# Five gathers moved within GpSimd's order in the second step of a graph layer

## The chip, the cores and the metric

The kernel runs on one core of a Trainium2 chip. The core has five engines that each work through their own instruction queue: TensorE (PE, matrix products; its weight loads are listed as PEld), VectorE (DVE), ScalarE (ACT), GpSimd (POOL) and SyncE (SP, which here only issues DMAs). Queues wait for one another by semaphores. The metric is the device time of one execution in microseconds (us), the median of several runs.

## The reference

One layer of a graph network on 3327 nodes with 256 features each. `adj` is a sparse 3327 x 3327 matrix with a diagonal.

```python
h = relu(layernorm(x))
R = adj + I;  R = R / R.sum(-1, keepdims=True)
Xf = Xa = h;  Z = 0
for n in range(2):
    A  = top_p_attention(Xa, W1, W2, W3)    # softmax rows; the largest entries up to a sum
    Xf = R @ Xf                             # of 0.9 are kept and scaled to sum 1
    Xa = A @ Xa
    Z  = Z + Xf @ U1[n].T + Xa @ U2[n].T
out = x + layernorm(h + Z) * ln_g + ln_b
```

The costly part is the attention: for each of 3327 rows of 3327 probabilities, the threshold above which the kept entries hold 0.9 of the row's sum has to be found.

## The kernel before, in words

Nodes are cut into NT = 26 tiles of 128 rows (P). The two steps of the reference are the two rounds of the loop `for step in range(2)` (from L1112), and within a step the loop over `i` runs from -1 to 27. In iteration i several tiles are worked on at once, each at another stage. A stage is a Python generator, and each `yield` ends one piece of it. A table of letters says how the pieces are woven: an iteration has seven parts (PARTS), and for each part a string names the stages whose next piece is emitted, letter by letter (L1158, L1159). `PLAN[1]` is the second step's table; `OPEN` replaces it for the first iterations (-1 to 3) and `LAST` for the last ones (25 to 27). The instruction order on PE, ACT and DVE is pinned to the order of this text, and from the start of the second step that of POOL too (L1183 to L1188). SP's is not.

The stages that matter here, in the second step:

- `w`, `q`: `weights`, the logits of a tile (PE, L597) and their exponentials (ACT, L601, L605) into a tile `e` of 128 x 3328.
- `m` and, from the next iteration on, `n`: `measured_twice` for tile i+1, which guesses the threshold (called the guess's chain here). Its pieces: (A) small ACT operations and two on POOL, L673 and L674; (B) a pass over the whole `e` on ACT (`through`, L630); (C) a second such pass; (D, the middle part) DVE L681, L682, ACT L683 to L685, then POOL L686, L687, L688; (E) a third pass on ACT; (F) POOL L693, L694, DVE L695, L696, ACT L698 to L701, DVE L703, L704, POOL L705, L706; (G) ACT L708, an exponential scaled by the column that L706 writes; (H) DVE L710, L711, which write the guess. A to F are emitted in iteration i as `m`, in parts 0, 1, 3, 4, 5 and 6; G and H in parts 1 and 2 of the next iteration as `n`.
- `d`, `c`: `settle` for tile i, on DVE: one operation over the whole tile that compares `e` with the guess (L725), 20 searches for the eight largest of a segment (L730), the search over the candidates (L734 to L749), and one operation over the whole tile that cuts `e` at the threshold (L759). L725 and L759 each read two SBUF inputs and take 3.69 us.
- `g`: `fetching`, the chain of `refetch(t)` over all tiles. For a tile it issues on SP one load of the packed adjacency blocks (`ac`, L1088), and on POOL five indirect DMAs (L897, "gathers") that fetch rows of `vx` into `xg`. Each call of `g` issues one gather, the first one of a tile also the load. `ac` and `xg` have two buffers.
- `s`: `spread` for tile i, which multiplies `ac` with `xg` on PE (L905) and adds on DVE (L1080).
- `f`: `finish`, the layer norm of a finished tile; on POOL L462, L463, L937 (the reciprocal deviation) and, one iteration later, L945 to L947.
- `sums.turn` and `sums.sum` transpose the cut `e` (PE L805, ACT L807) and multiply it with the features (PE L819).

In iterations 4 to 23 the gathers of iteration i are for tile i+2. Twelve gathers are issued in iterations -1 and 0, and in iterations 1 to 3 there is a sixth one in part 5 (`mgdf`), so that the 130 gathers end in iteration 23. POOL's order in an iteration of the second step is: L673, L674, L945 to L947, the five gathers, L686 to L688, L462, L463, L937, L693, L694, L705, L706.

Of the kernel before, what the change touches and what calls it, by code (L numbers as in the profile page):

```python
# [344 lines left out]
def guess_graph_layer(ctx, tc, x, adj, w1t, w2t, w3t, u1t, u2t, ln_g, ln_b, out, flag):  # L345
# [740 lines left out]
    def refetch(t):  # L1086
# [7 lines left out]


    PLAN = (("mdsssa", "mcdsssa", "edawwp", "msda", "mpdea", "gdwwq", "emgq"),
            ("llcmss", "lnms", "lwwnfd", "lcmdsssggggg", "fsmwqdf", "llmdf", "lmwd"))

    LAST = {NT - 1: ("cfss", "cn", "nd", "sss", "fdddddsf", "f", ""), NT: ("c", "", "", "ff", "ff", "fv", "f"),
            NT + 1: ("fv", "f", "", "", "f", "f", "f")}  # L1100
    OPEN = {-1: ("llcmss", "lnms", "lwwnfd", "lcmdsssggggg", "fmgswqdf", "llmdf", "lmwfdm"),
            0: ("cmssggg", "nms", "wwnfd", "cmdsss", "fsmgwqdf", "mdf", "mwd"),
            1: ("cmss", "nms", "wwnfd", "cmdsssggggg", "fsmwqdf", "mgdf", "mwd")}
    OPEN[2] = OPEN[3] = OPEN[1]
    fetching = itertools.chain(*(refetch(t) for t in range(NT)))
    LATE = (1, 4)
# [81 lines left out]
@with_exitstack  # L1188
def tile_graph_layer(ctx, tc, *args):
    keep = ctx.enter_context(tc.tile_pool(name="keep", bufs=1))  # L1190
    flag = keep.tile([1, 1], I32, tag="flag", name="flag")
    guess_graph_layer(tc, *args, flag)
    failed = tc.nc.values_load(flag[0:1, 0:1], min_val=0, max_val=1 << 20)
    with tc.If(failed > 0):
        search_graph_layer(tc, *args)
# [34 lines left out]
```

## Time and profile before

| | |
|---|---|
| median of 3 runs | 1404.44 us (1404.25 to 1408.04) |
| the profiled execution: its time / its span | 1405.77 us / 1404.0 us |
| mean granted TensorE clock | 0.981 |
| busy share of the span: PE, DVE, ACT, POOL | 91%, 85%, 79%, 57% |
| the 130 gathers of the second step (L897, `xg<-vx`) | 129.5 us busy, 996 ns each; idle before them 38.6 us |
| L673 in the second step, 23 occurrences with `law` | 46.4 us busy, 2017 ns each |
| L686, 25 occurrences | 267 ns each |
| L693, 25 occurrences | 258 ns each |
| L725 and L759 on the whole tile | 3.69 us each |

Lines of the profile read: an engine, the source line, the operation, output and inputs with their shapes, and a count; in the time line, the start in us from the beginning of the span, the length, and in brackets how long the engine sat idle before it and what ended that wait. "issue" is a time in which the engine waited for nothing that the profile shows. The chain of waits is the work that ended last, followed back from the end.

### The profile page before, as it was taken

The numbers are of one execution on the slowest core, as the hardware profiler recorded it, in microseconds if no ns is written. First come the engines' busy times: TensorE is split into PE (matmuls) and PEld (weight loads), VectorE is DVE, ScalarE is ACT, GpSimd is POOL, SyncE is SP. The second block draws the span as 40 slices with busy tenths as digits, with TensorE's granted clock in tenths as the row PEclk, the third lists the DMA queues.
The fourth block names the chain that finished last, engine by engine and source line by source line (L and its number), as shares of the span: only waits on it lengthen the run. The fifth ranks groups of instructions, "written<-read, shape, count | busy, mean of one in ns | idle before, by whom it ended". The sixth has DMA issues, their size and how long they took to land.

```text
span 1404.0 us, 22095 instructions
## 1 busy us (share of the span) xinstructions
PE 1275.7 (91%) x6495; PEld 976.9 (70%) x6495; DVE 1195.0 (85%) x3673; ACT 1105.3 (79%) x2451; POOL 795.3 (57%) x1243
## 2 busy tenths in 40 slices
PE   6897999999999999999999759999999999999985
PEld 5545777777767777777777537777777777777764
DVE  6878898898988979989882489999998999999993
ACT  5467777878877778778773689999998999999941
POOL 6225766666657656666673475655655555565522
PEclk9999999999999999999999879999999999999998
DMA  8884453444444534534422121322312223132200
GB/s 279 269 269 122 118 145 109 128 138 117 128 125 115 143 107 122 146 111 125 126 78 83 51 72 45 90 77 60 91 56 80 67 70 88 50 89 73 63 20 22
DMA packets 91203, 149.77 MB, mean 107 GB/s; under 512 B 15266, under 2 KB 58657, under 8 KB 91073
## 3 DMA queue, kind: packets, MB, share of 16 engines
q1 hardware_dynamic: 73616, 105.37, 23.8%
q0 software_dynamic: 16640, 42.69, 12.3%
q8 instruction: 54, 0.88, 0.3%
q14 instruction: 77, 0.62, 0.1%
q10 hardware_dynamic: 816, 0.20, 0.1%
HBM read 120.93 MB, written 27.28 MB: 106 GB/s over the span
## 4 chain that ended last, share of the span: by engine, by line
PE 43%; DVE 40%; ACT 11%; issue 4%; DMA 1%; POOL 1%; SPq 0%; another core or an unknown queue 0%; DVEq 0%; ACTq 0%; POOLq 0%
PE pa L819 18%; DVE cand L730 8%; DVE w L725 7%; PE pt L805 6%; DVE e L759 5%; PE pr L905 4%; PE pl L597 4%; DVE cand L739 3%; ACT ja L630 3%; DVE bb L737 3%; PE pz L982 3%; PE pz L918 3%; DVE x L759 2%; ACT eT L807 2%; PE pk L1023 1%
## 5 line engine op out<-in xcount | busy, mean ns | idle before, releaser
L819 PE MATMUL pa<-xw,eT 128*128 128x256 f32 x1352 | 323.6, 384 | 27.4 <-DVE s L929 26.2
L630 ACT ACTIVATE ja<-e,g 128x3328 uint8<-128x3328 f32 x106 | 325.7, 3073 | 0.1
L819 PE MATMUL pa<-x,eT 128*128 128x256 f32 x1352 | 325.2, 382 | 0.0
L819 PEld LDWEIGHTS pa<-xw,eT 128*128 128x128 f32 x1352 | 250.7, 190 | 77.9 <-DVE s L929 31.6
L807 ACT COPY eT<-pt 128x512 f32<-128x512 f32 (+1 forms) x364 | 200.6, 559 | 119.8 <-PE pt L805 100.5
L819 PEld LDWEIGHTS pa<-x,eT 128*128 128x128 f32 x1352 | 244.8, 192 | 26.3
L730 DVE MAX8 cand<-w 128x8 f32<-128x168 f32 (+1 forms) x1040 | 251.4, 317 | 0.0
L805 PE MATMUL pt<-ident,e 128*128 128x128 f32 x1144 | 176.1, 276 | 18.2 <-DVE e L756 9.1
L897 POOL DMA_INDIRECT xg<-bx,index x130 | 156.6, 1205 | 45.2 <-issue 31.5
L805 PEld LDWEIGHTS pt<-ident,e 128*128 128x128 f32 x1144 | 140.9, 144 | 57.7 <-issue 29.2
L725 DVE SCALAR_TENSOR_TENSOR w<-e,g 128x3328 f32<-128x3328 f32 x44 | 162.1, 3684 | 0.7
L888 POOL DMA_INDIRECT ac<-in_adj,index x130 | 130.3, 1002 | 44.5 <-issue 29.6
L897 POOL DMA_INDIRECT xg<-vx,index x130 | 129.5, 996 | 38.6 <-issue 38.6
L759 DVE SCALAR_TENSOR_TENSOR e<-e,rec 128x3328 f32<-128x3328 f32 x40 | 147.5, 3688 | 0.6
L905 PE MATMUL pr<-xg,ac 128*128 128x257 f32 (+1 forms) x520 | 140.6, 395 | 6.8 <-DVE s L1080 6.8
L601 ACT ACTIVATE e<-pl 128x832 f32<-128x832 f32 x132 | 113.8, 867 | 17.9 <-PE pl L597 14.4
L905 PEld LDWEIGHTS pr<-xg,ac 128*128 128x128 f32 x520 | 94.0, 194 | 32.1 <-issue 14.2
L737 DVE MAX8 bb<-cand 128x8 f32<-128x160 f32 x286 | 92.6, 324 | 6.4
L597 PE MATMUL pl<-after,qT 64*128 64x416 f32 x416 | 95.5, 553 | 0.0
L597 PE MATMUL pl<-both,qT 64*128 64x416 f32 x416 | 90.4, 538 | 0.8 <-DVE both L1000 0.8
L673 POOL TENSOR_SCALAR g<-g,law 128x1 f32<-128x1 f32 x23 | 46.4, 2017 | 67.4 <-ACT g L672 67.4
L922 POOL TENSOR_TENSOR sv<-sv,x 128x256 f32<-128x256 f32 x26 | 19.8, 763 | 109.9 <-ACT sv L921 109.9
(255 smaller groups left out, 2153.5 us busy)
## 6 DMA issues: line engine op xcount, KB each, us to landing
at<-in_adj SPq DMA_DIRECT2D x102, 256.0 KB
cx<-ac SPq DMA_DIRECT2D x26, 384.0 KB
ac<-cx SPq DMA_DIRECT2D x26, 384.0 KB
wide<-in_adj SPq DMA_DIRECT2D x10, 832.0 KB
e<-in_adj SPq DMA_DIRECT2D x8, 832.0 KB
bx<-e SPq DMA_DIRECT2D x26, 128.5 KB
own<-bx SPq DMA_DIRECT2D x26, 128.5 KB
x<-in_x SPq DMA_DIRECT2D x13, 256.0 KB
```

What stands on the lines that cost most here:

```text
L597: PE.matmul(pl[:, a, :wd], qT[p, :], keys_of(step, a).rearrange("p a b -> p (a b)")[:, c : c + wd], start=True, stop=True)
L630: S.activation(ja, e, f, bias=guess, scale=sign, accum_out=total)
L725: V.scalar_tensor_tensor(w, e, col(16), e, ALU.is_lt, ALU.mult, accum_out=d2)
L730: V.max(cand[:, 8 * s : 8 * s + 8], w[:, s * SEG : min(NP, (s + 1) * SEG)])
L737: V.max(b8, cand)
L759: V.scalar_tensor_tensor(e, e, at(1), e, ALU.is_ge, ALU.mult, accum_out=ra)
L805: PE.transpose(pt[:, j, :], e[:, (j0 + j) * P : (j0 + j + 1) * P], ident)
L807: S.copy(eT[:, :w, :], pt[:, :w, :])
L819: PE.matmul(self.pa, eT[:, c - 4 * k, :], self.xa[:, j, :], start=c == 0, stop=c == NT - 1)
L888: G.indirect_dma_start(out=ac[:, k, :], out_offset=None, in_=rows, in_offset=bass.IndirectOffsetOnAxis(ap=index[:, t, k : k + 1], axis=0), ...
L897: G.indirect_dma_start(out=xg[:, k, :w], out_offset=None, in_=rows, in_offset=bass.IndirectOffsetOnAxis(ap=index[:, t, k : k + 1], axis=0))
L905: PE.matmul(pr[:, :w], ac[:, k, :], own if k == KT - 1 else xg[:, k, :w], start=k == 0, stop=k == KT - 1)
```

## The change

The letters of the second step's table are rearranged. In `PLAN[1]` and in `OPEN[1]` (which also serves iterations 2 and 3) five `g` leave the end of part 3 and stand in part 4 behind `fsm`, that is behind piece D of the guess's chain. Nothing is added or taken away.

```diff
     PLAN = (("mdsssa", "mcdsssa", "edawwp", "msda", "mpdea", "gdwwq", "emgq"),
-            ("llcmss", "lnms", "lwwnfd", "lcmdsssggggg", "fsmwqdf", "llmdf", "lmwd"))
+            ("llcmss", "lnms", "lwwnfd", "lcmdsss", "fsmgggggwqdf", "llmdf", "lmwd"))
...
-            1: ("cmss", "nms", "wwnfd", "cmdsssggggg", "fsmwqdf", "mgdf", "mwd")}
+            1: ("cmss", "nms", "wwnfd", "cmdsss", "fsmgggggwqdf", "mgdf", "mwd")}
```

POOL's order in an iteration becomes: L673, L674, L945 to L947, L686 to L688, the five gathers, L462, L463, L937, L693, L694, L705, L706. The load of `ac`, which comes with a tile's first gather, moves with it in the text. The sixth gather of iterations 1 to 3 stays in part 5.

## The prediction

> **What bounds the kernel now.** I read the page's account by engine first, then the chain of waits, then the time line of one iteration of the second step. The chain over the whole span says that no single engine sets the time:
>
> ```profile
> PE 43%; DVE 40%; ACT 11%; issue 4%; DMA 1%; POOL 1%; SPq 0%; another core or an unknown queue 0%; DVEq 0%; ACTq 0%; POOLq 0%
> ```
>
> In the second step (from 787 us on) the chain runs on VectorE (DVE) with short visits to ScalarE (ACT). VectorE's two long operations and the one wait in between carry an iteration, here the chain's five longest pieces between 1010 and 1032 us:
>
> ```profile
> 1010.83 2.32 DVE cand L730 x10
> 1015.99 0.55 issue
> 1020.46 3.71 DVE e L759 x2
> 1024.88 3.71 DVE w L725 x2
> 1029.57 1.96 DVE cand L730 x8
> ```
>
> The period, from one L682 to the next (1010.61 to 1032.46), is 21.85 us. Of 22 us there PE is busy 20.96, ACT 21.01, DVE 20.47 and POOL (GpSimd) 12.31: three engines are nearly full and GpSimd has slack, but GpSimd's order is that of the text, so what counts is who is late behind what. The same iteration in the time line (start, length, engine, line):
>
> ```profile
> 1010.61 0.21 DVE L682 TENSOR_SCALAR g<-g,oa 128x1 f32<-128x1 f32 x1
> 1011.66 0.29 ACT L685 ACTIVATE g<-g 128x1 f32<-128x1 f32 x1
> 1014.66 0.95 POOL L897 DMA_INDIRECT xg<-vx,index  x1 [0.30 <-issue]
> 1015.66 0.26 POOL L686 TENSOR_SCALAR g<-g 128x1 f32<-128x1 f32 x1
> 1016.30 0.21 ACT L630 ACTIVATION_READ_ACCUMULATOR ja<-x,g 128x1 f32 x1
> 1016.61 0.25 POOL L462 TENSOR_SCALAR rstd<-mv 128x1 f32<-128x1 f32 x1
> 1016.61 0.27 DVE L695 TENSOR_SCALAR g<-oa,g 128x1 f32<-128x1 f32 x1 [0.62 <-issue]
> ...
> 1017.98 0.26 POOL L693 TENSOR_SCALAR g<-oa 128x1 f32<-128x1 f32 x1
> 1019.11 0.30 POOL L706 TENSOR_SCALAR g<-g 128x1 f32<-128x1 f32 x1
> 1020.46 3.69 DVE L759 SCALAR_TENSOR_TENSOR e<-e,rec 128x3328 f32<-128x3328 f32 x1
> 1022.39 1.97 POOL L673 TENSOR_SCALAR g<-g,law 128x1 f32<-128x1 f32 x1 [2.98 <-ACT g L672]
> 1022.46 0.29 ACT L708 ACTIVATE g<-g 128x1 f32<-128x1 f32 x1
> 1024.45 0.23 POOL L674 TENSOR_SCALAR g<-g 128x1 f32<-128x1 f32 x1
> 1024.58 0.27 DVE L711 TENSOR_SCALAR g<-g 128x1 f32<-128x1 f32 x1
> ```
>
> Three things are to be seen. First, L686 is ready when L685 ends (1011.95) but runs at 1015.66: the gathers in front of it cost it 3.7 us. That lateness is nearly free, since L695, which needs L686's column, starts 0.10 us after the accumulator read that ends the third pass (1016.51), and 0.69 us after L686's end: the pass releases it, not GpSimd. Second, GpSimd finishes the chain's last operation (L706, ends 1019.41) 1.05 us before VectorE begins L759. Third, L673, a 128x1 operation, takes 1.97 us when it falls under L759 and ends only 3.90 us after L759's start. The same line took 0.34 us at 791.02, clear of it, and averages 2.02 us over 23 occurrences: a small GpSimd operation that falls under the long two-input operation is held to its end.
>
> **The change, part by part.** Nothing is added or removed: five gathers (and the one load of `ac` on SP's queue that goes with the first) move in the text from ahead of L686-L688 to behind them. It applies to iterations 1 to 23, 23 of them (with 12 gathers issued before and six each in iterations 1 to 3, the 130 run out in iteration 23).
>
> *L686-L688 earlier.* They gain 3.7 us, worth nothing while the third pass releases L695. Only one iteration differs: at 1055.75 a gather began 2.65 us late, L686 ran at 1061.91 and L695 waited 2.52 us instead of 0.63. There the change gains 1.9 us in all.
>
> *The load on SP and the landing of the gathers.* A tile gathered in iteration i is read in iteration i+2, over a period later; both move some 3.5 us later. Cost nothing; the cover is over 20 us.
>
> *What now stands behind the gathers.* Two groups are queued after them: L462, L463, L937 (needed by L944 at 1028.34, 10 us after L937 ends) and L693, L694, L705, L706. L706 scales the exponential L708 on ScalarE, and behind L708 in ScalarE's order stand two 3.07 us passes of the next tile. I count from the end of L682 (1010.82 = 0):
>
> L686 at 1.24 (L685 ends at 1.13; where L686 is not queued it starts 0.11 after, 800.62 to 800.73). L688 0.60 later. First gather 0.53 after L688's start (801.33 to 801.86). Then 1.40 to the second, 3 x 1.255 to the fifth, 1.00 to the next operation (1009.50, 1010.90, 1014.66, 1015.66). L462 so starts at 8.53. L462 to L693 is 1.37: L693 at 9.90. L759 starts at 9.64 (1020.46), so L693 misses it by 0.26 us and is held: to 9.64 + 3.90 = 13.54. L694 0.09 later, 13.63, and 1.07 from there to L706's end (1018.34 to 1019.41): 14.70. L708 starts at 14.81 where it was at 11.64 (1022.46): 3.17 us late.
>
> What is late next: on VectorE, L711 waits for L708, at 15.14 instead of 13.76, 1.38 us. On ScalarE all is back to back from L708 to the end of the second pass of the next tile, 9.53 us (1022.46 to 1031.99): 24.34. Then L681 0.10 later and 0.45 to L682's end: 24.89. VectorE alone would be at L681 at about 22.9, so ScalarE decides. The new period is 24.89, **3.04 us more** than 21.85. PE has 4 us idle then and sets nothing.
>
> The spacing is the delicate choice. The Trainium skill (Perfetto Trace Analysis, GPSIMD Engine Instruction) says that reported spans of GpSimd do not add up and that the start-to-start spacing is to be used. The row shows both: 0.95 us long, 1.255 us apart. By spans the lengths from L686 to L706 add to 7.90 us, end at 9.14, before L759, and the change would cost nothing; by spacing they end at 11.33 without a hold. I go by spacing, since a start is when the next one really came.
>
> *Where the trace has no row* is a L693 that comes under L759 itself. Bounds: not held at all, L706 ends at 11.33 and L708 isn't late (0 us); held as L673 in all 23 occurrences, 3.04 us. L673 is the same kind (tensor-scalar, 128x1), so the upper end. Also unknown is which operation meets L759 first. If one is slower by 0.1 us it is L937 (+0.35 us a period); if the gathers come 1.1 us later it is L462, then 1.40 us more (L463 at 13.63 and 2.47 to L706's end, 16.10). That is what I take for iterations 2 and 3, where a sixth gather goes ahead of L462: 2 x 1.40 = 2.8. In the other direction, L759 could come later by waiting for a running GpSimd operation, at most the 0.26 us of L937.
>
> A second rule concerns gathers themselves. By the Trainium skill (SBUF — State Buffer, Who interferes with whom) a two-input VectorE operation takes only the shared read side, and descriptor writing is inferred not to be hindered by it. Here the gather that began at 851.41 under L725 (849.98 to 853.71) took 3.13 us instead of 0.95, though the one at 850.05 took 1.05. The row decides: gathers that slip under L759 would be held too. By the rule that would save up to 2.1 us in an iteration where it happens; in the forecast no whole gather lies there.
>
> **Sum.** 23 x 3.04 = 69.9; + 2.8; - 1.9: 70.8 us. The profiled execution took 1405.77 (span 1404.0), which gives 1476.6; the median of the runs is 1404.44, 1.3 less, so 1475.2. **I predict 1475 us**, 5.0% slower. A difference of 0.3% (4 us) is about what a measurement can tell from none.
>
> **The rivals.** *Not held, no change.* If a 128x1 operation that starts under L759 were not stopped, L706 ends at 11.33 and ScalarE reaches L708 at 11.64 as before; only the 1.9 us come back: 1402.5, the same. This decides as long as L706 ends before about 11.5. Against it: L673 ends 3.90 us after the start of L759 wherever it falls there; for it: only 0.26 us separate L693 from escaping, though L694 to L706 would still be caught. *GpSimd did hold L695.* Then the 0.55 us wait goes in 23 periods: 1404.4 - 12.7 - 1.3 = 1390. Against it: the 0.10 us after the pass. *VectorE alone is late.* If ScalarE had slack, each period would grow by VectorE's 1.38: 31.7 + 2.8 - 1.9, 1437. Against it: 21.01 of 22 us busy. *Everything caught.* If the gathers run later than counted, as the one that waited 2.65 us, L462 is the first held: 21 x 1.40 more, 1505; a lower PE clock in its longer idle times (1.00 now in these windows) would end there too.
>
> **How the numbers follow.** Forecast 0.69 (by itself 1463 to 1487, from which operation is held first); everything caught 0.13; VectorE alone 0.08; not held 0.08; GpSimd held L695 0.02. The time is the forecast's. The range, 1450 to 1500, leaves out the last three cases and the far half of the worse one, about 0.2. Faster by over 0.3%: 0.02, within: 0.08, slower: 0.90.
>
> **What would show it.** In the changed profile L686 starts 0.1 us after L685; the five gathers end about a microsecond before L759; L693 is some 3.6 us long and ends 3.9 us after L759's start; ScalarE waits about 3 us ahead of L708 for L706; VectorE waits at L681 for L630; the period is near 24.9 us and PE's waits grow. Wrong would be: L706 ended ahead of L759, L693 0.26 us long under it, or a period that grows by VectorE's part alone.

## The result, and the profile after

The changed kernel takes 1476.43 us in the median of 4 runs (1473.07 to 1479.73) against 1405.2 (1404.25 to 1408.04), now of 4 runs, for the one before: a ratio of 1.0503, 95% interval 1.0484 to 1.0521. The profiled execution took 1473.07 us (span 1471.3).

The chain of waits over the whole span, by engine, in the changed kernel:

```profile
PE 44%; ACT 26%; DVE 15%; POOL 10%; issue 4%; DMA 0%; another core or an unknown queue 0%; POOLq 0%; ACTq 0%; SPq 0%; DVEq 0%
```

VectorE's share fell from 40% to 15%, ScalarE's rose from 11% to 26% and GpSimd's from 1% to 10%: the second step now runs along other engines. Which ones wait for whom is told by the table of waits between 790 and 1400 us (us in total, times, longest):

```profile
ACT g L708 <- POOL g L706: 74.4, 23, 5.4
...
DVE g L681 <- ACT ja L630: 38.2, 24, 4.1
...
DVE g L711 <- ACT g L708: 22.4, 24, 1.3
...
DVE g L710 <- POOL g L694: 12.3, 22, 2.7
```

The first line is new: ScalarE stands 23 times, once in each of the iterations 1 to 23, 3.2 us on average, ahead of L708 for GpSimd's L706. VectorE's waits follow from the same lateness: at L711 for L708, at L710 for L694, which stands ahead of L706 on GpSimd, and at L681 for ScalarE's second pass. The time line of one iteration (L682 of this iteration ends at 1035.35) shows why L706 is late:

```profile
1042.89 0.95 POOL L897 DMA_INDIRECT xg<-vx,index  x1 [0.30 <-issue]
1043.92 0.25 POOL L462 TENSOR_SCALAR rstd<-mv 128x1 f32<-128x1 f32 x1
...
1044.93 0.26 POOL L937 TENSOR_SCALAR nm<-mv,rstd 128x1 f32<-128x1 f32 x1
1045.01 3.69 DVE L759 SCALAR_TENSOR_TENSOR e<-e,rec 128x3328 f32<-128x3328 f32 x1
1045.28 3.52 POOL L693 TENSOR_SCALAR g<-oa 128x1 f32<-128x1 f32 x1
...
1049.66 0.30 POOL L706 TENSOR_SCALAR g<-g 128x1 f32<-128x1 f32 x1
...
1050.00 0.29 ACT L708 ACTIVATE g<-g 128x1 f32<-128x1 f32 x1 [3.00 <-POOL g L706]
...
1059.56 0.21 DVE L681 TENSOR_SCALAR g<-oa,g 128x1 f32<-128x1 f32 x1 [1.50 <-ACT ja L630]
```

The fifth gather begins at 1042.89. L693 begins 0.27 us after L759 and takes 3.52 us instead of 0.26; it ends at 1048.80, 0.10 us after L759's 3.69 us. L706 ends at 1049.96, L708 starts 0.04 us later after a wait of 3.00 us, and at the end of the turn L681 waits 1.50 us for the second pass (L630 on ScalarE). The next L682 ends at 1060.02: a period of 24.67 us against 21.85.

To compare kernels I use, beside the whole time, the length from the end of L682 in iteration 1 to that in iteration 24, 23 periods that hold every moved gather. It is 504.73 us before (835.92 to 1340.65) and 571.11 after (835.64 to 1406.75), 66.38 more; the two profiled spans differ by 67.3. So all but 0.9 us of the loss lies there.

### The profile page after: what moved, and what is told of

Same layout as the page of the kernel before. It is cut to its first block, busy times and chain, and to the rows that moved or that the text cites. A ratio compares the mean times of both kernels' runs of the same rounds, so it can differ in the third digit from the quotient of the medians.

```text
span 1471.3 us, 22095 instructions
## 1 busy us (share of the span) xinstructions
PE 1304.4 (89%) x6495; PEld 984.6 (67%) x6495; DVE 1198.4 (81%) x3673; ACT 1106.9 (75%) x2451; POOL 826.6 (56%) x1243
## 4 chain that ended last, share of the span: by engine, by line
PE 44%; ACT 26%; DVE 15%; POOL 10%; issue 4%; DMA 0%; another core or an unknown queue 0%; POOLq 0%; ACTq 0%; SPq 0%; DVEq 0%
PE pa L819 18%; ACT ja L630 12%; PE pt L805 6%; PE pr L905 4%; POOL g L693 4%; PE pl L597 4%; ACT eT L807 4%; DVE cand L730 3%; PE pz L982 3%; PE pz L918 3%; ACT e L601 2%; DVE cand L739 2%; DVE bb L737 2%; DVE w L725 2%; POOL xg L897 2%
## 5 line engine op out<-in xcount | busy, mean ns | idle before, releaser
L819 PE MATMUL pa<-xw,eT 128*128 128x256 f32 x1352 | 338.1, 397 | 33.9 <-DVE s L929 33.9
L630 ACT ACTIVATE ja<-e,g 128x3328 uint8<-128x3328 f32 x106 | 325.7, 3073 | 0.1
L819 PEld LDWEIGHTS pa<-xw,eT 128*128 128x128 f32 x1352 | 260.3, 198 | 88.0 <-DVE s L929 39.6
L807 ACT COPY eT<-pt 128x512 f32<-128x512 f32 (+1 forms) x364 | 200.5, 558 | 119.2 <-PE pt L805 105.4
L725 DVE SCALAR_TENSOR_TENSOR w<-e,g 128x3328 f32<-128x3328 f32 x44 | 162.0, 3682 | 0.7
L759 DVE SCALAR_TENSOR_TENSOR e<-e,rec 128x3328 f32<-128x3328 f32 x40 | 147.5, 3687 | 0.6
L601 ACT ACTIVATE e<-pl 128x832 f32<-128x832 f32 x132 | 113.6, 866 | 17.1 <-PE pl L597 11.4
L945 POOL TENSOR_TENSOR s<-s,gam 128x256 f32<-128x256 f32 x25 | 18.2, 726 | 133.0 <-ACT s L944 133.0
```

What stands on the lines that cost most here:

```text
L601: S.activation(e.rearrange("p (a n) -> p a n", a=2)[:, :, c : c + wd], pl[:, :, :wd], AF.Exp, accum_out=za[:, n : n + 1])
L630: S.activation(ja, e, f, bias=guess, scale=sign, accum_out=total)
L725: V.scalar_tensor_tensor(w, e, col(16), e, ALU.is_lt, ALU.mult, accum_out=d2)
L759: V.scalar_tensor_tensor(e, e, at(1), e, ALU.is_ge, ALU.mult, accum_out=ra)
L807: S.copy(eT[:, :w, :], pt[:, :w, :])
L819: PE.matmul(self.pa, eT[:, c - 4 * k, :], self.xa[:, j, :], start=c == 0, stop=c == NT - 1)
```

## The experiments

The runs were made on other chips of the same kind, where the kernel before took 1390.12 us (the first four), 1394.68 (the next three) and 1366.38 (the last) instead of 1405, so the absolute times in the expectations are to be read as differences to the kernel before. The length of the 23 periods scatters far less: the control below, on another chip than the kernel before, has 504.40 us against 504.73.

| run | ratio to before, 95% interval | 23 periods, us (before 504.73) | period from iteration 4 on, median |
|---|---|---|---|
| the change | 1.0503, 1.0484 to 1.0521 | 571.11 | 24.68 |
| L759 with one input, changed order | 1.0009, 0.9981 to 1.0038 | 506.24 | 21.87 |
| L759 with one input, order of before | 1.0000, 0.9965 to 1.0036 | 504.40 | 21.85 |
| four gathers moved | 1.0278, 1.0222 to 1.0334 | 540.32 | 23.48 |
| three gathers moved | 1.0051, 1.0012 to 1.0090 | 508.68 | 21.85 |
| L708 behind the pass | 1.0356, 1.0276 to 1.0435 | 554.55 | 24.46 |
| iterations 1 to 3 alone | 1.0103, 1.0064 to 1.0143 | 515.44 | 21.85 |
| all behind L706 | 1.0015, 0.9974 to 1.0055 | 504.99 | 21.86 |
| behind L706 from iteration 4 | 0.9988, 0.9978 to 0.9998 | 502.88 | 21.85 |

**Is it the hold, or the order?** Both could make L706 late. L759 was given one SBUF input instead of two, in the second step:

```diff
-            V.scalar_tensor_tensor(e, e, at(1), e, ALU.is_ge, ALU.mult, accum_out=ra)
+            if step:
+                V.tensor_scalar(e, e, at(1), None, ALU.is_ge, ALU.add, accum_out=ra)
+            else:
+                V.scalar_tensor_tensor(e, e, at(1), e, ALU.is_ge, ALU.mult, accum_out=ra)
```

> The changed kernel, but in the second step the cut at the threshold (L759) is a tensor-scalar comparison that reads one SBUF input and sums what it writes; the kept entries become ones, so the output is not the reference's. Theory (a two-input VectorE operation holds the small GpSimd operations): L693 keeps its 0.26 us under L759, L706 ends at about 11.3 us after L682, L708 starts at 11.6 as before the change, and the period goes from 24.7 back to about 21.9 us: 1404 to 1410 us if the new form also takes 3.69 us. Rival (the order alone: what stands behind five gathers is late, held or not): the period stays near 24.7 and the time near 1476 us.

> The control: the kernel before with the same one-input L759 in the second step, so the output is not the reference's. Both theories: within 5 us of 1405 us if the form takes 3.69 us; L673 alone gets short under L759 (0.34 instead of 2 us). If the form is faster, this run says by how much, and the run with the changed order is to be read against this one.

In the time line of the first run the operation is as long as before (3.68 us; it is now on line 760), and the small ones run through beneath it, to be read against L693 above:

```profile
1026.95 3.68 DVE L760 TENSOR_SCALAR_CACHE_REDUCE x<-x,rec 128x3328 f32<-128x3328 f32 x1
1027.22 0.25 POOL L693 TENSOR_SCALAR g<-oa 128x1 f32<-128x1 f32 x1
...
1028.34 0.31 POOL L706 TENSOR_SCALAR g<-g 128x1 f32<-128x1 f32 x1
...
1028.83 0.29 ACT L708 ACTIVATE g<-g 128x1 f32<-128x1 f32 x1
```

L693 begins 0.27 us after the long operation, as in the changed kernel, and takes 0.25 us. The period is back at 21.87 and the ratio at 1.0009, with five gathers still in front. The control's ratio is 1.0000, so the form itself gains nothing, and L673, which lies under it, has come down to 341 ns from 2017. Of the 66.38 us, the hold makes 571.11 - 506.24 = 64.9; the order alone makes the remaining 1.5, in iterations 2 and 3, where the sixth gather makes L706 end at 12.5 and 12.6 us after L682, later than ScalarE needs it.

The changed kernel with two inputs and with one also shows the hold on a gather. In iteration 11 the first gather comes late in both, so the fifth begins 0.10 us after L759. In the changed kernel:

```profile
1094.34 3.69 DVE L759 SCALAR_TENSOR_TENSOR x<-x,rec 128x3328 f32<-128x3328 f32 x1
1094.44 4.40 POOL L897 DMA_INDIRECT xg<-vx,index  x1 [0.30 <-issue]
```

With one input (the gather's line is L900 there):

```profile
1048.79 3.68 DVE L760 TENSOR_SCALAR_CACHE_REDUCE x<-x,rec 128x3328 f32<-128x3328 f32 x1
1048.89 0.95 POOL L900 DMA_INDIRECT xg<-vx,index  x1 [0.30 <-issue]
```

The same gather at the same place takes 0.95 us instead of 4.40.

**A threshold, or so much a gather?** Four and three of the gathers were moved:

```diff
-  "lcmdsss", "fsmgggggwqdf", "llmdf", "lmwd"     (the change, part 3 to 6)
+  "lcmdsssg", "fsmggggwqdf", "llmdf", "lmwd"     (four moved; OPEN[1] alike)
+  "lcmdsssgg", "fsmgggwqdf", "llmdf", "lmwd"     (three moved; OPEN[1] alike)
```

> Four of the five gathers behind L686 to L688, one ahead. Theory (what counts is who is still to run when L759 begins at 9.64 us): L706 comes up at 9.77, is held to 13.45, L708 is 1.9 us late, the period of iterations 4 to 23 is about 23.5 us: 1440 to 1448 us. Rival (each gather moved costs its own 1.25 us of delay, in proportion): four fifths of 71 us, 1462 us.

> Three of the five gathers behind L686 to L688, two ahead. Theory: L706 ends at 8.8 us, before L759 begins at 9.64, so nothing is held from iteration 4 on and only iterations 2 and 3 with their sixth gather and the one iteration with a late gather pay 1.7 us each: 1403 to 1409 us, no slower than before. Rival (in proportion): three fifths of 71 us, 1448 us.

With four, from the time line of one iteration:

```profile
1024.52 3.69 DVE L759 SCALAR_TENSOR_TENSOR e<-e,rec 128x3328 f32<-128x3328 f32 x1
1024.55 3.75 POOL L706 TENSOR_SCALAR g<-g 128x1 f32<-128x1 f32 x1
...
1028.33 0.29 ACT L708 ACTIVATE g<-g 128x1 f32<-128x1 f32 x1 [1.80 <-POOL g L706]
```

From iteration 4 on, but for iteration 11, L693, L694 and L705 are through when L759 begins; only L706 is caught, by 0.03 us, and that is enough: L708 waits 1.80 us, the period is 23.48 and the 23 periods 35.6 us longer. The median is 40 us above before, inside what was expected (35 to 43 above 1405). With three, L706 ends at 8.73 us after L682, L759 begins at 9.64, and the median period from iteration 4 on is 21.85; the 3.95 us over before come from iterations 2 and 3 (1.65 and 1.68) and from iteration 11 (0.60). The ratio, 1.0051, is above what was expected at most, but its interval reaches down to 1.0012. In proportion to the gathers it would have been 1.040 and 1.030. It is a threshold: the end of the last operation that the chain needs, against the beginning of L759.

**Who carries the delay on?** In the changed kernel two letters were swapped, so that ScalarE's next pass goes ahead of L708:

```diff
-  PLAN[1]: "llcmss", "lnms", ...     OPEN[1]: "cmss", "nms", ...
+  PLAN[1]: "llcmss", "lmns", ...     OPEN[1]: "cmss", "mns", ...
```

> The changed kernel with two letters swapped in part 1 (mn for nm): ScalarE runs the next tile's first pass (L630, 3.07 us) ahead of L708 instead of behind it. Theory (the loss is ScalarE standing still for L706 with two passes queued behind; VectorE alone would lose 1.3 us a period): ScalarE's wait ahead of L708 shrinks from about 3 us to under 0.3, VectorE still waits at L711, the period is about 23.2 us: 1435 to 1443 us. Rival (GpSimd's own order sets the period, whoever waits for it): L706 ends no earlier, the period stays 24.7 and the time near 1476 us.

Half hit. L706 comes no earlier, and yet every other period is 23.35 us, so GpSimd's order by itself doesn't set it; ScalarE waits for L706 in 4 iterations instead of 23, 4.2 us in all, and VectorE waits at L711 for L708 (24.8 us in 23 times). But the periods between are about 24.5, and the whole is 49.8 us longer than before, not 30 to 38. The time line shows PE at the beginning of a long period and of a short one:

```profile
1127.93 3.66 PE L819 MATMUL pa<-xw,eT 128*128 128x256 f32 x8 [2.42 <-DVE s L929]
...
1152.64 1.99 PE L819 MATMUL pa<-xw,eT 128*128 128x256 f32 x8 [2.10 <-DVE s L929]
```

The same eight products take 3.66 us after an idle time of 2.42 us and 1.99 after 2.10. The busy times by window carry the clock in the column behind POOL (then the DMA share and GB/s):

```profile
1122.00:1125.00 3.00, 3.00 (x18) 2.37 (x17) 2.93 (x5) 3.00 (x5) 1.55 (x2) 1.00 0.29 73
1125.00:1128.00 3.00, 0.58 (x5) 0.26 (x2) 3.00 (x13) 1.89 (x3) 1.25 (x2) 0.99 0.33 115
1128.00:1131.00 3.00, 3.00 (x7) 2.46 (x8) 2.96 (x14) 1.97 (x6) 0.76 (x3) 0.50 0.42 123
1131.00:1134.00 3.00, 3.00 (x18) 2.50 (x16) 2.59 (x12) 1.93 (x2) 2.36 (x3) 0.94 0.16 44
```

For 3 us PE was granted half its clock. The waits behind it read as a chain: ScalarE's copy L807 waits 1.30 us for the transposes, the third pass behind it begins late, and L695 waits for that pass:

```profile
1132.07 0.58 ACT L807 COPY eT<-pt 128x512 f32<-128x512 f32 x1 [1.30 <-PE pt L805]
...
1135.82 0.27 DVE L695 TENSOR_SCALAR g<-oa,g 128x1 f32<-128x1 f32 x1 [2.02 <-ACT ja L630]
```

In the next period the clock stays at 1.00, L695 waits 0.62 us, and the two kinds alternate. Why the clock falls in one and not in the other isn't shown, and the length of the last idle time alone doesn't decide it: in the changed kernel the same eight products took 1.99 us at one time and 3.68 at another after the same idle time.

```profile
1008.36 1.99 PE L819 MATMUL pa<-xw,eT 128*128 128x256 f32 x8 [1.33 <-DVE s L929]
1033.05 3.68 PE L819 MATMUL pa<-xw,eT 128*128 128x256 f32 x8 [1.32 <-DVE s L929]
```

**Does it build up?** The move in `OPEN[1]` alone, with `PLAN[1]` as before:

> The move in iterations 1 to 3 alone; from iteration 4 on the order of before. Theory: these three periods cost 2.3, 4.1 and 4.1 us as in the changed kernel, where the sixth gather puts L462 first under L759: 10.5 us, 1416 us. Rival (the cost builds up from one iteration to the next): under 1410 us.

The periods of iterations 1 to 3 are 24.16, 26.01 and 26.02 us, as in the changed kernel (24.17, 26.00, 26.01), then 22.14 and from there 21.85 (but for iteration 11). That is 10.7 us over before, as expected; the ratio of 1.0103 holds 10.5 us within its interval. Nothing builds up; each iteration pays for itself.

**Gathers last.** All gathers behind L706, first in all iterations, then from iteration 4 on alone:

```diff
-  "lcmdsss", "fsmgggggwqdf", "llmdf", "lmwd"
+  "lcmdsss", "fsmwqdf", "llmdf", "lmgggggwd"     (OPEN[1]: "cmdsss", "fsmwqdf", "mdf", "mggggggwd")
```

> All gathers behind L706, at the end of part 6. Theory: L706 ends at about 8.3 us, before L759, so nothing that the chain needs is held; the gathers themselves run into L759 and L725 and are held there (one some 4 us long), which delays L673, L945 to L947 but not past their need: 1402 to 1408 us. Rival (GpSimd gets too full when its gathers are held twice, and L686 of the next iteration comes late): L686 later than 5.5 us after L682 and over 1415 us.

> From iteration 4 on all five gathers behind L706, as in the run before this one; iterations 1 to 3 in the order of before, since there the gathers have less lead and PE waited 2 us for one. Theory: no period longer than before, and the iteration with the late first gather no longer holds L695 (1.5 us won): the second step from the first to the 24th L682 takes 503.2 us against 504.73 before; the whole time 0.1% less, which the runs can hardly tell from none. Rival (something else of the late gathers costs): over 504.7 us.

In the first of these runs L706 ends at 7.6 us after L682, and it is the gathers that are caught:

```profile
1002.69 0.94 POOL L897 DMA_INDIRECT xg<-vx,index  x1 [0.31 <-issue]
1002.89 3.69 DVE L759 SCALAR_TENSOR_TENSOR e<-e,rec 128x3328 f32<-128x3328 f32 x1
1003.94 3.46 POOL L897 DMA_INDIRECT xg<-vx,index  x1 [0.30 <-issue]
...
1007.31 3.69 DVE L725 SCALAR_TENSOR_TENSOR w<-x,g 128x3328 f32<-128x3328 f32 x1
1007.70 4.12 POOL L897 DMA_INDIRECT xg<-vx,index  x1 [0.30 <-issue]
```

The one that began before L759 takes 0.94 us, the next 3.46, and one under L725 4.12. Nobody needs them soon, and the period is 21.86. Iteration 1 loses 2.0 us, since its gathers have less lead there and PE waited 2.00 us for one; iteration 11, the one with a late first gather, wins 1.9 back, of which iteration 12 loses 0.4, since the held gathers run on into it. With iterations 1 to 3 left as they were the 23 periods take 502.88 us, 1.85 less than before, and the ratio is 0.9988, 0.9978 to 0.9998: 0.1% less than the kernel before, at the edge of what the runs can tell.

## Why the prediction was right, point by point

- **L686 to L688 earlier, worth nothing.** Right. L686 starts at 1.24 us after L682, as worked out, and L695 at 5.79, as before.
- **The gathers' places.** Right to 0.05 us: worked out 2.37, 3.77, 5.03, 6.28, 7.53 after L682, measured 2.39, 3.79, 5.04, 6.29, 7.54. Start-to-start spacing was the right measure; by the spans L693 would have been early enough.
- **Who meets L759 first.** L693, as taken, in 17 of the 23 iterations (1, 4 to 10, 13, 15 to 22). In 2 and 3 it is L462, as taken too. In 14 and 23 it is L937, the case named at +0.35 us; in 14 it made the period 24.96 us, 0.3 longer than its neighbours. Outside the account are iteration 11 (the fifth gather) and 12 (L694, after L693 slipped through). The margin of 0.26 us was measured as 0.27.
- **The hold.** Right in kind, and now shown: with one input it is gone. Its size was 0.1 us too long (L693 ends at 13.45, not 13.54).
- **ScalarE decides.** Right: L708 at 14.65 instead of 14.81, 0.09 us from the shorter hold and 0.07 because it starts 0.04 us after L706 and not the 0.11 I took; from there 10.02 us to L682's end, where I had 10.08. So a period grows by 2.83 us where 3.04 was the term. The swap of L708 and the pass points the same way: every other period shrank to 23.35 us though L706 came no earlier.
- **Iterations 1 to 3, and 23.** Iteration 1 was mis-sized at 3.04: it grew by 2.27. No tile is finished yet there, so L944 (0.60 us, of which 0.5 until the next operation starts) isn't in ScalarE's queue, which I hadn't taken out. Iterations 2 and 3 grew by 4.15 and 4.12 where 4.44 was said, with L462 caught first, as taken. Iteration 23 grew by 1.29 instead of 3.04: the two exponentials L601 of a further tile are no longer in ScalarE's queue, L681 shows no wait for ScalarE, and what is left is close to VectorE's own 1.38.
- **The 1.9 us given back.** Wrong, in sign. I had let L686 go free of the late gather and forgotten that all that stands behind the gathers now takes the lateness instead. In iteration 11 the first gather came late again: GpSimd stood idle ahead of it for 2.48 us where 0.28 is usual. The fifth began 0.10 us after L759 and took 4.40 us, L706 ended at 17.01 us after L682, and the period was 27.07 us; before it was 23.75, and 24.89 was the forecast. Even without the hold little would have come back: with one input in L759 the period of iteration 11 is 23.62. The step failed where it stopped at the first instruction that profits and did not follow the late one to the end of its queue.
- **PE sets nothing.** Right on the whole, but its clock did not stay at 1.00: it was 0.57 between 1034 and 1037 us, and over the span 0.969 instead of 0.981. The periods around that place are 24.69 and 24.67 us, like the others; in iterations 4 and 12 (0.50 to 0.55 between 908 and 914 us, 0.50 between 1109 and 1115) L695 came 0.16 and 0.33 us late, and only the period of iteration 4 shows it, 24.82.
- **The sum.** 70.8 us was said; the 23 periods grew by 66.4 and the spans by 67.3. The errors partly cancel: the 18 iterations from 4 to 22 without 11 grew by 2.85 on average instead of 3.04 (3.5 us less in all), 1 to 3 by 1.4 less and 23 by 1.75 less than said, iteration 11 by 2.2 more. The median grew by 71.2, so its nearness to the predicted 1475 is partly luck: the four runs lie 6.7 us apart and the profiled one, 3.5 us below the 1476.6 said for it, is the fastest.
- **The rivals.** "Not held" fell with L693's 3.52 us, "GpSimd held L695" with its unchanged start, "VectorE alone" with the period of 24.68. What "Everything caught" describes, L462 or what stands ahead of it held first, happened in iterations 2, 3 and 11 alone.

## What to carry to other kernels

When work is moved within the queue of an engine that has slack, follow what then stands behind it to the end of that queue and ask which long operation of another engine begins meanwhile: a delay of 2.7 us was free up to that moment and put 3.3 us on top past it (L706 ends at 14.61 us after L682; unheld, with one input in L759, at 11.36; before at 8.6). Long transfers that nobody needs soon belong behind the last small operation that someone does need, as long as they keep their lead (in iteration 1 PE waited 2.00 us for one). Where an expected gain comes from freeing one waiter, put the same lateness on whoever is next in the queue before counting it.

## What the runs showed of the hardware

- A gather on GpSimd that begins 0.10 to 1.4 us after a two-input VectorE operation is held too: 3.13 to 4.40 us instead of 0.95, and 0.95 again when the operation has one input. The Trainium skill (SBUF — State Buffer, Who interferes with whom) infers that descriptor writing isn't hindered by such an operation; these rows show the gather as a whole held, and for this kernel they decide. Which part of it is held, the reading of its index or the writing of its descriptors, was not tried, so the inference itself is neither shown nor refuted.
- Starts that lie under 0.1 us apart in the profile don't tell who is held. L706 that began 0.03 us after L759 was held; in one iteration of the changed kernel L693 began 0.05 us after it and was not (0.25 us long), and L694 behind it was held instead, for 3.44 us; a gather that began 0.07 us after L725 in the kernel before (850.05) took 1.05 us.
- PE's clock fell to 0.50 for about 3 us after an idle time of 2.42 us and did not after 2.10 in the run with L708 behind the pass; but in the changed kernel it fell to 0.57 behind an idle time of 1.32 us. What decides it stays open.
- In all ten profiles the first gather of iteration 11 begins 2.2 to 2.6 us later than that of its neighbours, with nothing in the profile that it waits for that explains it. The cause stays open.
